# Attention with a gated feed-forward on one Trainium2 core: statistics turned at a unit's end and sent a unit sooner, row masks behind both kinds of scores

## The chip, the cores and the metric

The kernel runs on one core of a Trainium2 chip. A core has five engines with a queue each: TensorE (PE) multiplies matrices, VectorE (DVE) and ScalarE (ACT) work element by element and can read what PE wrote in PSUM, [...] and SyncE (SP) issues DMAs. [...] The metric is the time of one execution on the device, in microseconds (us); lower is better.

## What is computed

The reference, cut to what matters (16 sequences of 512 tokens, width 128, 16 heads with keys of 8 and values of 64 numbers, all fp32):

```python
xn = layernorm(x)
# attention
q = (xn @ Wq), k = (xn @ Wk), v = (xn @ Wv)          # split into 16 heads
scores = einsum('bhqd,bhkd->bhqk', q, k) / sqrt(8)
scores = where(causal, -inf, scores)                  # a query sees itself and earlier keys
attn = softmax(scores, axis=-1)
a = (attn @ v).reshape(B, T, 1024) @ Wo
# feed-forward
xr = mu_r * xn + (1 - mu_r) * shifted(xn)
xk = mu_k * xn + (1 - mu_k) * shifted(xn)
f = sigmoid(xr @ W_r.T) * (relu(xk @ W_k.T)**2 @ W_v.T)
out = x + a + f
```

## The kernel before

Every softmax is done with two kinds of scores. **Row scores** (tile `sm`, queries on the partitions) serve the statistics alone: DVE takes each row's negated maximum `negm`, ACT takes exp of the row with that maximum as bias and sums it into `z`, and takes the logarithm of the sums into `lz`. **Turned scores** (tile `sT`, keys on the partitions) serve the products with v: their matmul has 35 rows instead of 33, the two more being the statistics `negm - log z` of each query, split into a high and a low part (`mh`, `ml`) and written as two more rows of q. So `sT` comes out of PE already normalised, ACT takes its exp into `e`, POOL sets the diagonal blocks' masked half to zero, and PE multiplies with v (`weigh`, tile `av`), after which DVE copies the context out (`take_ctx`) and PE projects it (`project_out`, tile `po`).

The work is cut into units. A **group** is a batch's two pairs of heads and makes five units, t = 0 to 4, in which the blocks of 512 x 512 causal scores are dealt out [...] (`ROWS` L301 for the row scores, `KEYS` L309 for the turned ones, `WEIGHED` L317 for the products). A batch has four groups, so 20 units; 16 batches make 320. The function `unit_work(n)` (L531) issues one unit; it runs three groups' places at once. `now` is unit n, whose turned scores, exp and products are done. `stat_now` is unit n + 10 (`LEAD`), whose row sums ACT takes. `stat_next` is unit n + 11, whose row scores, masks and maxima are made.

Nothing but this order decides what runs when: `_InOrder` (L32) records each engine's instructions in program order, and each engine takes them one after another. In a unit the order is: send statistics (`put_stats` L409, four DMAs on POOL's queue that write `mh` and `ml` into q's rows), row scores (`rowscores` L328), their masks (`rowmask` L341, small bf16 matmuls that add -3e38 above the diagonal), turned scores (`scores` L424), the turn (`turn_stats` L398: PE transposes `lz` into `pm`, DVE makes `mh` and `ml`), a context copy, the maxima (`rowmax` L359), the row sums (`rowsum` L378) and, in a group's last statistics unit, the logarithm (`log_sums`), then exp and masks of `e` (`weights` L435), then side work and `weigh`. Side work comes from a table by unit number (`at` L492): the next batches' normalisation, projections of q, k and v, the feed-forward, the spreading of q and k over partitions by DMAs on SP's queue (`spread_qk` L232) and the output. Where t is 1, side work comes behind `weigh`, else ahead of it.

For a group whose row sums end in unit n (t = 4), the logarithm is taken in n, the subtraction `lz = negm - log z` (`sub_logs`, DVE) is the last piece of side work of n + 1, the turn is in n + 2 and the sending in n + 3. The turned scores that read the statistics begin in unit n + 6. With units of a batch numbered 0 to 19, the subtraction is in units 0, 5, 10 and 15, the turn in 1, 6, 11, 16, the sending in 2, 7, 12, 17.

Buffers that bind units to each other: `sm` has two PSUM buffers, so row scores wait for the row sums two units before; `sT` has one, so turned scores wait for the exp of the unit before; `av` has one, and the side products and `pm` share one tile `m`.

Side work that stands near the turns, in the middle of the run: unit 0 `ffn_r` (PE `pr`, DVE `e_sig`), unit 4 `y`, `deviation`, unit 5 a v projection, unit 9 the output `o` and `mix` (`xmix`), unit 10 the projection of q for the batch after next (DVE `qh`, `ql`), unit 14 a v projection and `mix`, unit 15 that of k (`kh`, `kl`). The last two batches have no batch after next and lack the q, k and normalisation pieces.

Of the kernel before, what the change touches and what calls it, by code (L numbers as in the profile page):

```python
# [47 lines left out]
def attn_ffn_kernel(  # L48
# [101 lines left out]
    def m_tile(name):  # L150
        n = lent[0] % 3 if lent else 0
        if lent:
            lent[0] += 1
        if n == 1:
            return ps_av.tile([P, T], FP, tag="av", name=name)
        if n == 2:
            return ps_st.tile([P, 2, 512], FP, tag="sT", name=name)[:, 0, :]
        return ps_m.tile([P, 512], FP, tag="m", name=name)
# [160 lines left out]
    def unit_of(n):  # L319

        n, t = divmod(n, UNITS)
        b, g = divmod(n, NPAIR // 2)
        return (b, g, t) if 0 <= b < B else None
# [4 lines left out]
    def rowscores(b, g, t):  # L328
        q, k = qs[b % 2], ks[b % 2]
        sm = sms[b, g, t] = ps_sm.tile([P, 2, 512], FP, tag="sm", name=f"sm_{b}_{g}_{t}")  # L330
        for w, i, to in ROWS[t]:
            n = (i + 1) * P
            for u in range(2):
                s = slice(64 * u, 64 * u + RS)

                pe.matmul(
                    sm[:, u, to : to + n], q[s, 2 * g + w, i * P : n], k[s, 2 * g + w, :n],
                    start=(to == 0), stop=False,
                )

    def rowmask(b, g, t):  # L341

        ends = [to + (i + 1) * P for _, i, to in ROWS[t]]
        step = ends[-1] - ends[0] or P
        for c in range(2):
            for u in range(2):
                s = slice(64 * u, 64 * u + 64)
                cols = sms[b, g, t][:, u, ends[0] - P :]
                if len(ends) > 1 and step > P:
                    cols = cols.rearrange("q (m k) -> q m k", k=P)[:, 0 :: step // P, 64 * c :]  # L350
                else:
                    cols = cols.rearrange("q (m k) -> q m k", k=P)[:, :, 64 * c :]
                pe.matmul(
                    cols, id64[s, c, :],
                    mask64[s, c : c + 1, 64 * c :].to_broadcast([64, len(ends), P - 64 * c]),
                    start=False, stop=(c == 1),
                )
# [20 lines left out]
    def rowsum(b, g, t):  # L378
        negm, z = stats[b, g]
        sm = sms.pop((b, g, t))  # L380
        for w, i, to in ROWS[t]:
            for u in range(2):
                cols = sm[:, u, to : to + (i + 1) * P]
                act.activation(
                    cols, cols, AF.Exp,
                    bias=negm[:, u, w, i : i + 1], accum_out=z[:, u, w, i : i + 1],
                )

    def log_sums(b, g):
        lz = stat.tile([P, 2, 2, NB], FP, tag="lz", name=f"lz_{b}_{g}")  # L390
        act.activation(lz, stats[b, g][1], AF.Ln)
        stats[b, g] += (lz,)
# [5 lines left out]
    def turn_stats(b, g):  # L398

        lz = stats.pop((b, g))[2]  # L400
        pm = m_tile(f"pm_{b}_{g}")[:, 0:P]
        pe.transpose(pm[0 : 4 * NB], lz.rearrange("q u p i -> q (u p i)"), ident)
        hi = stat.tile([4 * NB, P], FR, tag="mh", name=f"mh_{b}_{g}")
        lo = stat.tile([4 * NB, P], FR, tag="ml", name=f"ml_{b}_{g}")
        dve.tensor_copy(hi, pm[0 : 4 * NB])
        dve.tensor_tensor(lo, pm[0 : 4 * NB], hi.bitcast(FP), ALU.subtract)
        stats[b, g] = (hi, lo)

    def put_stats(b, g):  # L409

        for n, half in enumerate(stats.pop((b, g))):
            for u in range(2):
                r = 64 * u + RS + n
                pool.dma_start(
                    out=qs[b % 2].bitcast(FP)[r : r + 1, 2 * g : 2 * g + 2, :].rearrange(
                        "o p (i t) -> o (p i) t", t=P
                    ),
                    in_=half.bitcast(FP)[2 * NB * u : 2 * NB * u + 2 * NB],
                )
# [4 lines left out]
    def scores(b, g, t):  # L424
        q, k = qs[b % 2], ks[b % 2]
        st = sts[b, g, t] = ps_st.tile([P, 2, 512], FP, tag="sT", name=f"sT_{b}_{g}_{t}")
        for w, j, to in KEYS[t]:
            for u in range(2):
                s = slice(64 * u, 64 * u + RA)
                pe.matmul(  # L430
                    st[:, u, to : to + T - j * P], k[s, 2 * g + w, j * P : (j + 1) * P],
                    q[s, 2 * g + w, j * P : T], start=(to == 0), stop=(to + T - j * P == 512),
                )
# [28 lines left out]
    def take_ctx(b, p):  # L462
        c = ctxp.tile([P, T], FP, tag="ctx", name=f"ctx_{b}_{p}")
        dve.tensor_copy(c, avs.pop((b, p)))
        ctxs[b, p] = c
# [24 lines left out]
    todo, turns, puts = {}, {}, {}  # L490

    def at(n, f, *args):  # L492
        todo.setdefault(n, []).append((f, args))
# [4 lines left out]
    for b in range(B):  # L498
        n0 = b * per
        if b + 1 < B:  # L500
            r = 0 if b else 7
            at(n0 + r, ffn_r, b + 1)
            at(n0 + r + 1, ffn_exp, b + 1)
            for c, n in enumerate((3, 8, 13, 18) if b else (11, 13, 14, 18)):
                at(n0 + n, ffn_sig, b + 1, c)
            for m, n in enumerate((1 if b else 3, 5, 12, 13, 14, 16, 17, 18)):
                at(n0 + n, project_v, b + 1, m // 2, m % 2)
            at(n0 + 7, mix_prev, b + 1, 1)
            at(n0 + 9, mix, b + 1, 1)
            at(n0 + 11, ffn_k, b + 1)  # L510
            at(n0 + 19, ffn_out, b + 1)
            for m, n in enumerate((-3, -1, 0, 1, 4, 5, 5, 6) if b else (0, 0, 1, 1, 4, 5, 5, 6)):
                at(n0 + n, spread_qk, b + 1, *SPREAD[m], slice(0, NPAIR // 2))
            for m, n in enumerate((6, 9, 9, 10, 10, 11, 14, 14)):
                at(n0 + n, spread_qk, b + 1, *SPREAD[m], slice(NPAIR // 2, NPAIR))
        if b + 2 < B:
            at(n0 + 4, deviation, b + 2)
            for c in range(NB):
                at(n0 + (1, 1, 3, 3)[c], row_moments, b + 2, c)
                at(n0 + 4 + c // 2, normalise, b + 2, c)  # L520
            at(n0 + 6, transpose_xn, b + 2)
            at(n0 + 10, project_qk, b + 2, False)
            at(n0 + 15, project_qk, b + 2, True)
            at(n0 + 12, mix_prev, b + 2, 0)
            at(n0 + 14, mix, b + 2, 0)
        for p, n in enumerate((2, 3, 3, 4, 7, 8, 8, 9) if b < B - 1 else (-8, -7, -7, -6, -3, -2, 0, 3)):
            at(n0 + per + n, project_out, b, p)
        if b + 3 < B:
            at(n0 + 11, load_x, b + 3)

    def unit_work(n):  # L531
        now, stat_now, stat_next = (unit_of(n + m) for m in (0, LEAD, LEAD + 1))
        if n in puts:
            put_stats(*puts.pop(n))
        if stat_next:
            rowscores(*stat_next)
            rowmask(*stat_next)
        if now:
            scores(*now)
        if n in turns:  # L540
            turn_stats(*turns.pop(n))
        t = n % UNITS
        done = {0: (n - UNITS, 0), 2: (n - UNITS, 1)}.get(t)
        if done and unit_of(done[0]):
            b, g, _ = unit_of(done[0])
            take_ctx(b, 2 * g + done[1])
        if stat_next:
            rowmax(*stat_next)

        if stat_now:  # L550
            rowsum(*stat_now)
            b, g, kind = stat_now
            if kind == UNITS - 1:
                log_sums(b, g)
                at(n + 1, sub_logs, b, g)
                turns[n + 2] = puts[n + 3] = b, g
        if now:
            weights(*now)
        pieces = todo.pop(n, ())
        if t != 1:  # L560
            for f, args in pieces:
                f(*args)
        since, w, blocks = WEIGHED[t]
        if unit_of(n - since):
            b, g, _ = unit_of(n - since)
            for j in blocks:
                weigh(b, 2 * g + w, j, (t, j) in ((1, 3), (4, 3)))
        if t == 1:
            for f, args in pieces:
                f(*args)  # L570

    halves = {}

# [84 lines left out]
    for n in range(first - 1, B * per + 2):  # L658
        if n == -1:
            lent.clear()  # L660
        unit_work(n)
# [35 lines left out]
```

## Time and profile before

| | |
|---|---|
| median of 3 runs (lowest, highest) | 1035.7 us (1035.53, 1037.13) |
| the profiled execution | 1035.34 us, of it 1033.5 us span |
| TensorE clock granted | 0.976 |
| ACT: exp of `sT` into `e`, x320 | 324.5 us, 1014 ns each |
| ACT: exp of the rows, x1024, and reading out their sums | 513.4 us and 201.3 us |
| DVE: maxima, x448 | 397.2 us |
| PE: products with v, x2048 | 338.3 us (modelled ends) |
| PE: row masks, x1280 | 101.0 us (modelled ends, overlapping) |
| PE: `pm`, x64; DVE: `mh`, `ml`, x64 each | 17.8 us; 17.8 us, 17.8 us |
| POOL: sending `mh` and `ml`, x128 each | 70.7 us and 66.1 us, 4 KB each, 1.7 and 1.6 us to landing (median) |
| SP: spreads of q and k, x124 each | 128 KB each, 4.8 and 5.1 us to landing (median) |

The span runs from the first to the last instruction of the program; the profiled execution's own time is 1.84 us longer. All kernel code is recorded under line 42, the helper that opens the pools, so instructions are told apart by tile names: `sm<-k,q` are row scores, `sm<-mask,id` their masks, `sm<-sm,negm` the row sums, `e<-sT` the exp of turned scores. In a timeline a row gives start, duration, engine, operation, tiles and shapes, how many were merged, and in brackets how long the engine stood idle before it and what ended that.

### The profile page before, as it was taken

The numbers are of one execution on the slowest core, as the hardware profiler recorded it, in microseconds if no ns is written. First come the engines' busy times: TensorE is split into PE (matmuls) and PEld (weight loads), VectorE is DVE, ScalarE is ACT, GpSimd is POOL, SyncE is SP. The second block draws the span as 40 slices with busy tenths as digits, with TensorE's granted clock in tenths as the row PEclk, the third lists the DMA queues.
The fourth block names the chain that finished last, engine by engine and source line by source line (L and its number), as shares of the span: only waits on it lengthen the run. The fifth ranks groups of instructions, "written<-read, shape, count | busy, mean of one in ns | idle before, by whom it ended". The sixth has DMA issues, their size and how long they took to land.

```text
span 1033.5 us, 23971 instructions
## 1 busy us (share of the span) xinstructions
PE 976.3 (94%) x8771; PEld 527.6 (51%) x8771; DVE 793.9 (77%) x1316; ACT 923.9 (89%) x2449; POOL 514.1 (50%) x957
## 2 busy tenths in 40 slices
PE   3789999999999999999999999999999999999997
PEld 1344464555546455554645555464554646455454
DVE  4787879688887878787797877878787797877741
ACT  0788999899999999999899999999999999999982
POOL 4165454544646464463645545564464546444432
PEclk8778999999999999999999999999999999999999
DMA  7722515034250512525043252504324150432000
GB/s 193 136 28 49 99 34 112 15 73 84 59 98 19 114 29 73 85 59 98 3 108 50 58 100 50 97 14 107 50 58 90 34 102 4 110 37 48 3 12 11
DMA packets 59971, 67.17 MB, mean 65 GB/s; under 512 B 12928, under 2 KB 33024, under 8 KB 59856
## 3 DMA queue, kind: packets, MB, share of 16 engines
q1 hardware_dynamic: 48688, 61.89, 30.8%
q0 software_dynamic: 8640, 1.34, 1.1%
q10 hardware_dynamic: 2528, 2.43, 0.9%
q8 instruction: 70, 1.15, 0.5%
q14 instruction: 45, 0.37, 0.2%
HBM read 39.13 MB, written 25.17 MB: 62 GB/s over the span
## 4 chain that ended last, share of the span: by engine, by line
PE 49%; ACT 32%; DVE 11%; issue 4%; DMA 3%; POOL 1%; POOLq 0%; ACTq 0%
ACT sm L42 22%; PE av L42 14%; ACT e L42 10%; PE po L42 10%; PE sm L42 8%; PE sT L42 7%; DVE negm L42 6%; DMA q<-ml 3%; PE pv L42 3%; PE pq L42 2%; PE pk L42 2%; PE pr L42 1%; PE pm L42 1%; DVE mh L42 1%; DVE ml L42 1%
## 5 line engine op out<-in xcount | busy, mean ns | idle before, releaser
L42 ACT ACTIVATE sm<-sm,negm 128x384 f32<-128x384 f32 (+3 forms) x1024 | 513.4, 501 | 78.1 <-DVE negm L42 29.3
L42 DVE TENSOR_REDUCE negm<-sm 128x2 f32<-128x768 f32 (+3 forms) x448 | 397.2, 909 | 77.8 <-PE sm L42 77.8
L42 POOL TENSOR_SCALAR_AFFINE_SELECT e<-e 128x256 f32<-128x256 f32 x512 | 203.5, 416 | 457.1 <-ACT e L42 454.5
L42 ACT ACTIVATE e<-sT 128x1024 f32<-128x1024 f32 x320 | 324.5, 1014 | 18.5 <-PE sT L42 18.2
L42 PE MATMUL av<-e,v 128*64 128x512 f32 (+3 forms) x2048 | 338.3, 441 | 1.1 <-DVE ctx L42 0.5
L42 PEld LDWEIGHTS av<-e,v 128*64 128x64 f32 x2048 | 138.7, 138 | 166.5 <-issue 130.7
L42 ACT ACTIVATION_READ_ACCUMULATOR sm<-sm,negm 128x1 f32 x1024 | 201.3, 197 | 0.0
L42 PE MATMUL sT<-q,k 35*128 35x512 f32 (+3 forms) x1024 | 164.0, 366 | 23.5 <-ACT e L42 13.9
L42 PE MATMUL sm<-k,q 33*128 33x384 f32 (+3 forms) x1024 | 164.0, 378 | 8.3 <-ACT sm L42 8.3
L42 PEld LDWEIGHTS sm<-k,q 33*128 33x128 f32 x1024 | 83.1, 188 | 169.0 <-ACT sm L42 89.3
L42 PE MATMUL pv<-wv,xnT 128*64 128x512 f32 x512 | 139.0, 622 | 1.5 <-DVE ffn L42 0.9
L42 PE MATMUL po<-wo,ctx 128*64 128x128 f32 x2048 | 133.2, 277 | 1.6 <-DVE ctx L42 1.6
L42 PEld LDWEIGHTS po<-wo,ctx 128*64 128x64 f32 x2048 | 109.8, 137 | 18.6 <-issue 7.8
L42 PEld LDWEIGHTS sT<-q,k 35*128 35x128 f32 x1024 | 86.6, 189 | 49.0 <-ACT e L42 36.8
L42 PE MATMUL sm<-mask,id 64*128 64x128 bf16 (+2 forms) x1280 | 101.0, 236 | 0.0
L42 DVE COPY ctx<-av 128x512 f32<-128x512 f32 x128 | 87.3, 682 | 16.0 <-PE av L42 15.9
L42 DVE COPY v<-pv 128x512 f32<-128x512 f32 x128 | 86.0, 672 | 4.3 <-PE pv L42 0.6
L42 DVE CAST mh<-pm 16x128 fp32r<-16x128 f32 x64 | 17.8, 278 | 79.3 <-PE pm L42 79.3
L42 POOL DMA_DIRECT2D q<-mh x128 | 70.7, 555 | 12.9 <-DVE mh L42 7.6
L42 POOL DMA_DIRECT2D q<-ml x128 | 66.1, 521 | 0.0
L42 DVE RECIPROCAL sig<-e_sig 128x128 f32<-128x128 f32 x64 | 60.2, 941 | 0.0
L42 POOL TENSOR_SCALAR prev<-xnT,omm 128x512 f32<-128x512 f32 x32 | 50.2, 1567 | 14.0 <-DVE xmix L42 14.0
(65 smaller groups left out, 599.4 us busy)
## 6 DMA issues: line engine op xcount, KB each, us to landing
q<-q SPq DMA_DIRECT2D x124, 128.0 KB, 4.8
k<-k SPq DMA_DIRECT2D x124, 128.0 KB, 5.1
k<-kh SPq DMA_DIRECT2D x30, 256.0 KB, 2.6
x<-in_L_attn_x_dram SPq DMA_DIRECT2D x16, 256.0 KB, 2.9
q<-qh SPq DMA_DIRECT2D x16, 256.0 KB, 4.2
q<-ql SPq DMA_DIRECT2D x16, 256.0 KB, 4.3
out_dram<-o SPq DMA_DIRECT2D x16, 256.0 KB, 2.8
k<-kl SPq DMA_DIRECT2D x15, 256.0 KB, 2.0
```

What stands on the lines that cost most here:

```text
L42: return self._tc.keep_in_program_order(f(*args, **kwargs))
```

## The change

Three edits in `unit_work` and one in the side work's table. The row masks of unit n + 11 are issued behind the turned scores of unit n instead of ahead of them. The turn is issued at the very end of a unit, behind side work and products with v, and one unit sooner: in units 0, 5, 10 and 15 of a batch, the unit in which `sub_logs` stands. The sending comes one unit sooner too, at the start of units 1, 6, 11 and 16. And the spreads of q and k are given other units of the table.

```diff
-            for m, n in enumerate((-3, -1, 0, 1, 4, 5, 5, 6) if b else (0, 0, 1, 1, 4, 5, 5, 6)):
+            for m, n in enumerate((-1, -1, 0, 0, 4, 4, 5, 5) if b else (0, 0, 0, 0, 4, 4, 5, 5)):
                 at(n0 + n, spread_qk, b + 1, *SPREAD[m], slice(0, NPAIR // 2))
-            for m, n in enumerate((6, 9, 9, 10, 10, 11, 14, 14)):
+            for m, n in enumerate((8, 9, 9, 10, 10, 14, 14, 15)):
                 at(n0 + n, spread_qk, b + 1, *SPREAD[m], slice(NPAIR // 2, NPAIR))
...
         if n in puts:
             put_stats(*puts.pop(n))
+
         if stat_next:
             rowscores(*stat_next)
-            rowmask(*stat_next)
         if now:
             scores(*now)
-        if n in turns:
-            turn_stats(*turns.pop(n))
+        if stat_next:
+            rowmask(*stat_next)
...
                 log_sums(b, g)
                 at(n + 1, sub_logs, b, g)
-                turns[n + 2] = puts[n + 3] = b, g
+                turns[n + 1] = puts[n + 2] = b, g
...
         if t == 1:
             for f, args in pieces:
                 f(*args)
+        if n in turns:
+            turn_stats(*turns.pop(n))
```

## The prediction

> **What bounds the kernel now.** I read the page first, then the waits of the even stretch 100 to 990 us, then the timelines of ACT, DVE and PE around one turn of the statistics, and last the stretches of lost clock. A batch is 20 units and takes 60.2 us (unit 140's statistics-scores start at 484.21 us is disturbed, so I count from unit 160 at 547.81 to unit 180 at 607.99). I number units inside a batch 0 to 19; the turns before the change stand in units 1, 6, 11 and 16.
>
> The page gives the busy times:
> ```profile
> PE 976.3 (94%) x8771; PEld 527.6 (51%) x8771; DVE 793.9 (77%) x1316; ACT 923.9 (89%) x2449; POOL 514.1 (50%) x957
> ```
> PE looks like the bound, but its ends are modelled. The waits between engines (engine and tile that waited, what released it, us in total, times, longest) say more:
> ```profile
> DVE mh L42 <- PE pm L42: 68.8, 58, 3.2
> ...
> ACT sm L42 <- DVE negm L42: 20.8, 52, 0.9
> ...
> ACT e L42 <- PE sT L42: 5.1, 4, 2.3
> PE sT L42 <- DMA q<-ml: 4.5, 4, 2.0
> ```
> ACT waits in only two ways: 52 times for a row maximum, and a few times for scores whose statistics landed late. Between these it runs without a gap, so ACT sets the pace and PE waits about 0.5 us per group of five units, nearly all of it ahead of sT. ACT's timeline at unit 11 and 12 of batch 7 (start, us, then the idle time before in brackets):
> ```profile
> 523.34 1.01 ACT L42 ACTIVATE e<-sT 128x1024 f32<-128x1024 f32 x1
> 524.79 0.56 ACT L42 ACTIVATE sm<-sm,negm 128x384 f32<-128x384 f32 x1 [0.43 <-DVE negm L42]
> ```
> The missing maximum is that of unit 11. DVE's timeline shows why it is late:
> ```profile
> 516.53 1.29 DVE L42 TENSOR_REDUCE negm<-sm 128x2 f32<-128x768 f32 x2 [1.47 <-PE sm L42]
> 517.85 0.69 DVE L42 TENSOR_TENSOR o<-po,y 128x512 f32<-128x512 f32 x1
> 518.46 0.74 DVE L42 SCALAR_TENSOR_TENSOR xmix<-xnT,mus,prev 128x512 f32<-128x512 f32 x1
> 519.12 0.69 DVE L42 COPY ctx<-av 128x512 f32<-128x512 f32 x1
> 519.72 1.22 DVE L42 TENSOR_REDUCE negm<-sm 128x2 f32<-128x1024 f32 x1
> 520.85 0.68 DVE L42 CAST qh<-pq 128x512 fp32r<-128x512 f32 x1
> 521.56 0.69 DVE L42 TENSOR_TENSOR ql<-pq,qh 128x512 fp32r<-128x512 f32 x1
> 522.17 0.29 DVE L42 TENSOR_TENSOR lz<-negm,lz 128x16 f32<-128x16 f32 x1
> 522.97 0.28 DVE L42 CAST mh<-pm 16x128 fp32r<-16x128 f32 x1 [0.50 <-PE pm L42]
> 523.28 0.28 DVE L42 TENSOR_TENSOR ml<-pm,mh 16x128 fp32r<-16x128 f32 x1
> 523.49 1.27 DVE L42 TENSOR_REDUCE negm<-sm 128x2 f32<-128x768 f32 x2
> ```
> mh and ml stand ahead of the maximum and wait for pm. But lz, which pm turns, ends only at 522.47: from 516.53 to there DVE had no gap. And PE, on the same stretch:
> ```profile
> 521.74 0.50 PE L42 MATMUL sm<-k,q 33*128 33x384 f32 x4
> 522.09 0.34 PE L42 MATMUL sm<-mask,id 64*128 64x256 bf16 x4
> 522.24 0.48 PE L42 MATMUL sT<-q,k 35*128 35x256 f32 x4
> 522.65 0.28 PE L42 MATMUL pm<-ident,lz 128*16 128x128 f32 x1
> ```
> PE is through unit 10's products at 521.74, 0.73 us before lz is there. Today sm, masks and sT fill that time; the change puts pm exactly there. Last, unit 0 of batch 7, and the clock behind it (window; PE, PEld, DVE, ACT, POOL busy; clock; DMA share; GB/s):
> ```profile
> 486.76 0.96 PE L42 MATMUL sT<-q,k 35*128 35x512 f32 x2 [1.96 <-DMA q<-ml]
> ```
> ```profile
> 489.00:491.00 2.00, 2.00 (x10) 0.49 (x6) 0.57 (x2) 1.29 (x4) 0.33 (x1) 0.50 0.33 99
> ```
>
> [...] the maximum of unit 11 had its masks by 522.5 and still stood behind mh until 523.49. [...] here the 1.96 us stop was followed by a granted 0.50, while a stop of 1.27 us before the scores at 424.73 left it at 1.00. [...]
>
> **The change part by part.** Frame: the times of batch 7; ACT's free pace from one e's end to the next is 3.17, 2.39, 3.17, 2.40, 3.41 us for units 5k to 5k+4.
>
> 1. Row masks behind sT. The masks themselves cost PE 0.10 to 0.15 (516.15 to 516.30), unchanged in sum. But the maximum needs them: it starts 0.38 after the first mask (516.15, 516.53), and now sT (0.41: 516.30 to 516.71) stands between. So every maximum is possible 0.41 later than today, and where sT waits for the e before it (single sT buffer), the masks no longer fill that wait, which leaves PE 0.10 to 0.17 behind. Units whose maximum has slack of 0.7 us or more before ACT wants it hide this themselves; where DVE has no gap up to lz it passes on.
>
> 2. The turn (pm 0.21 of PE; mh and ml 0.60 of DVE) moves from the middle of unit 5k+1 to the end of unit 5k, behind the weigh. Same instructions. Gained: the maximum of 5k+1 no longer waits for a pm behind its own sT. Added: pm waits for lz of the same unit, and behind pm on PE stand the next unit's sm, sT and masks, that is ACT's next e and its next maximum. From pm's start to that maximum's start it is 0.21 + 0.35 (sm) + 0.41 + 0.38 = 1.35; mh and ml (pm + 0.31 + 0.60) hide in it.
>
>  Group at unit 10 (q of batch b+2 projected): unit 9's sm at 515.95 (0.15 behind), sT 516.30, masks 516.71, maximum 517.09 instead of 516.53. DVE is full, so lz ends at 522.47 + 0.56 = 523.03. pm 523.07, while PE is there at 521.89: 1.18 us stall. Maximum 524.42 to 525.69, row sums at 525.71 instead of 524.79: **+0.92**.
>  Group at unit 15 (k): today lz 537.05, PE free 536.72, maximum 538.47. sT waits for e; the masks behind it put unit 15's maximum at sT 533.92 + 0.79 = 534.71, so 535.92, kh and kl to 537.25, lz 537.43, pm 537.48 (stall about 0.65), maximum 538.83: **+0.37**.
>  Group at unit 0: lz 551.32, PE free 551.72. Unit 0's maximum at sT 548.90 + 0.79, ends 550.90, e_sig and lz to 551.7; no stall. pm 551.82, maximum 553.17 instead of 553.45; ACT's wait of 0.22 on average (3.3 us over 15 batches in unit 2) falls by **0.1**.
>  Group at unit 5: unit 4's maximum 501.46 becomes 501.87; y, mv, ve, ctx, maximum, v, lz have no gap, so lz 507.00, pm 507.05 against PE at 506.67; maximum 508.40 instead of 508.42: **0**.
>  Sum: +1.2 us per batch. Bounds: +0.6 if the maximum loses only sT's own 0.29 in the chain of waits and PE regains its 0.15; +1.6 if the unit 5 and unit 0 groups slip by 0.2 each too.
>  It holds for the 14 batches that project for b+2: +16.8. The last two have no q, k or xmix there and lose their ACT waits of about 0.23 four times: -1.
>
> 3. Sent a unit sooner. POOL's four DMAs (2.1 us) go ahead of the masking of unit 5k+1's e instead of 5k+2's; that e is first weighed two units later, so the place costs nothing (if not, up to 0.5 us a group). For the group read at unit 0 the sending comes about 1.8 us sooner (ml is ready only after pm at 537.5), and the lateness beyond the usual wait of 0.68 was at most 1.5. So ACT's waits for sT in units 0 and 1 (2.13, 2.33, 0.30, 0.14 us), half-clock stretches included, should go: -5. Bounds 0 and -5.4.
>
> 4. Spreads on SP: the same 16 of 128 KB per batch, regrouped; one q joins the three issued at unit 19 or 0. They are needed nine units after the first half and four after the second, 12 us or more against 5 us of landing: 0. [...] a spread in ml's way is inside the bounds of 3.
>
> Sum: +16.8 - 1 - 5 = +10.8 on the profiled execution's 1035.34 us (span 1033.5 and 1.84 around it) gives 1046.1; the median of the runs is 0.36 above it, so about 1047. Differences below 0.2% (2 us) can't be told from none here.
>
> **The rivals.**
> (a) Faster: the masks' delay is taken up. If PE stands early enough at units 4, 9 and 14 that the maximum still starts when today's does, lz stays where it is: unit 5's group gains its 0.43, unit 0's 0.22, unit 15's nothing, unit 10's still loses 0.36 (pm at 522.5). -0.3 x 14 - 1 - 5 = -10, 1026. For it: the DVE gaps of 0.81 and 1.47 us before these maxima. Against it: those gaps end exactly 0.38 after the mask, so PE decides them, and PE has no slack there. It decides from the point where unit 9's masks come within 0.1 us of today. At its best all of 20.8 + 5.1 us goes: 1010.
> (b) The new 1.2 us stop at unit 10 takes the clock down as the 1.96 us stop did; two such places cost ACT about 2 us each. 14 times gives 1075, half of them 1061. Against: 1.27 us did not do it.
> (c) The gains and losses meet: +0.4 per batch is +5.6 and meets the -6, so 1034 to 1038. For: step 2's lower bound of +0.6 is near.
> That the sending is not sooner at all, since lz holds it, would leave out the -5: 1052, inside the forecast's range.
>
> **How the numbers follow.** Forecast (1038 to 1058, at 1047) 0.56; (b) or longer stalls 0.11; (c) 0.07; (a) 0.26. Below 1020 I leave about 0.11 of (a), above 1061 about 0.08. Slower takes the forecast, (b) and a sliver of (c): 0.68; same 0.05; faster 0.27.
>
> **What would show it.** Right: PE idle before pm released by lz, near 1.2 us at unit 10 and 0.65 at unit 15; "ACT e waits for sT" growing from 5 us (unit 11); the wait of mh for pm falling to about 0.3 each; no PE wait for ml. Wrong: ACT's wait for negm falling below 10 us with no PE wait for lz, or a period below 60 us per batch.

## The result, and the profile after

The changed kernel takes 1032.49 us (median of 11 runs, 1031.75 to 1033.74) against 1037.13 us (11 runs, 1033.52 to 1038.42) for the one before: ratio 0.9961, 95% interval 0.9951 to 0.9971. It is faster by 0.4%, where 1.1% slower was forecast. Its profiled execution took 1032.25 us with a span of 1030.5, so 3.0 us of span are gone. ACT's work is the same:

```profile
PE 961.6 (93%) x8771; PEld 525.6 (51%) x8771; DVE 792.8 (77%) x1316; ACT 923.9 (90%) x2449; POOL 520.3 (50%) x957
```

The waits between engines in the same stretch as before, 100 to 990 us (total, times, longest):

```profile
DVE mh L42 <- PE pm L42: 29.3, 59, 0.7
...
PE pm L42 <- DVE lz L42: 20.0, 28, 1.0
...
ACT sm L42 <- DVE negm L42: 13.4, 27, 0.8
...
ACT e L42 <- PE sT L42: 7.1, 14, 0.7
```

mh's wait for pm fell from 68.8 to 29.3 us, PE's wait for lz is new, ACT waits less for maxima (20.8 to 16.1: the 13.4 shown and 2.7 in unit 7 that the view puts down to PE's xnTp; in batch 7 the maximum ended 0.1 us before ACT went on), and its wait for scores in unit 1 has become one in unit 11. The line for ml is gone. DVE's timeline around the same turn, units 9 to 11 of batch 7:

```profile
513.49 1.29 DVE L42 TENSOR_REDUCE negm<-sm 128x2 f32<-128x768 f32 x2 [1.14 <-PE sm L42]
...
516.55 1.22 DVE L42 TENSOR_REDUCE negm<-sm 128x2 f32<-128x1024 f32 x1
517.68 0.68 DVE L42 CAST qh<-pq 128x512 fp32r<-128x512 f32 x1
518.40 0.69 DVE L42 TENSOR_TENSOR ql<-pq,qh 128x512 fp32r<-128x512 f32 x1
519.00 0.17 DVE L42 TENSOR_TENSOR lz<-negm,lz 128x16 f32<-128x16 f32 x1
519.62 0.28 DVE L42 CAST mh<-pm 16x128 fp32r<-16x128 f32 x1 [0.45 <-PE pm L42]
519.94 0.28 DVE L42 TENSOR_TENSOR ml<-pm,mh 16x128 fp32r<-16x128 f32 x1
520.53 1.29 DVE L42 TENSOR_REDUCE negm<-sm 128x2 f32<-128x768 f32 x2 [0.31 <-PE sm L42]
```

and PE's:

```profile
512.48 0.50 PE L42 MATMUL sm<-k,q 33*128 33x384 f32 x4
512.82 0.45 PE L42 MATMUL sT<-q,k 35*128 35x384 f32 x4
513.11 0.34 PE L42 MATMUL sm<-mask,id 64*128 64x256 bf16 x4
513.38 1.09 PE L42 MATMUL po<-wo,ctx 128*64 128x128 f32 x16
...
516.94 1.46 PE L42 MATMUL av<-e,v 128*64 128x512 f32 x8
519.32 0.27 PE L42 MATMUL pm<-ident,lz 128*16 128x128 f32 x1 [0.92 <-DVE lz L42]
```

The reader is to see two things. PE stands idle for 0.92 us ahead of pm at unit 10's end, where 1.18 was forecast, and the next maximum comes after it. But the masks start only 0.29 us after sT (512.82 to 513.11), not 0.41, so unit 9's maximum starts 1.01 us after its row scores (512.48 to 513.49) where it was 0.73 before (515.80 to 516.53).

Where the 3 us went is best seen from the times between the last exp of one batch and of the next, read from the two traces (the lead-in is what runs before batch 0's own units):

| us | before | after | difference |
|---|---|---|---|
| lead-in and batch 0 | 119.78 | 121.05 | +1.3 |
| batches 1 to 13 | 792.48 | 790.16 | -2.3 |
| of these, the shortest | 60.16 | 60.70 | +0.5 |
| of these, the longest | 63.60 | 61.36 | -2.2 |
| batch 14 | 60.29 | 58.88 | -1.4 |
| batch 15 and end | 60.94 | 60.46 | -0.5 |

An undisturbed batch, one whose statistics landed in time, became slower, 60.17 to 60.73. Before, batches 2 and 7 took 63.24 and 63.60 us and several others 60.4 to 61.2; after, batches 1 to 12 lie between 60.70 and 60.76 and only batch 13 takes 61.36. Against 13 times 60.17 the kernel before lost 10.3 us to such batches. From 489 to 491 us, where the kernel before was granted a clock of 0.50, the changed one was granted 1.00 (the clock is the third number from the end, then come DMA share and GB/s):

```profile
489.00:491.00 2.00, 2.00 (x24) 1.05 (x20) 1.61 (x4) 1.97 (x6) 1.78 (x5) 1.00 0.41 121
```

### The profile page after: what moved, and what is told of

It reads as the page before. It is cut to its first block, busy times and chain, and to the rows that moved or that the text cites. A ratio compares the mean times of both kernels' runs of the same rounds, so it can differ in the third digit from the quotient of the medians.

```text
span 1030.5 us, 24120 instructions
## 1 busy us (share of the span) xinstructions
PE 961.6 (93%) x8771; PEld 525.6 (51%) x8771; DVE 792.8 (77%) x1316; ACT 923.9 (90%) x2449; POOL 520.3 (50%) x957
## 4 chain that ended last, share of the span: by engine, by line
PE 57%; ACT 19%; DVE 17%; issue 6%; POOL 1%; DMA 0%; ACTq 0%; DVEq 0%; POOLq 0%
PE av L42 16%; ACT sm L42 13%; PE sm L42 12%; PE po L42 10%; DVE negm L42 7%; PE sT L42 7%; ACT e L42 6%; PE pv L42 6%; DVE sig L42 2%; PE pr L42 1%; DVE v L42 1%; PE pm L42 1%; PE pkv L42 1%; DVE xmix L42 1%; PE xnTp L42 1%
## 5 line engine op out<-in xcount | busy, mean ns | idle before, releaser
L42 POOL TENSOR_SCALAR_AFFINE_SELECT e<-e 128x256 f32<-128x256 f32 x512 | 208.2, 426 | 418.2 <-ACT e L42 416.0
L42 PE MATMUL sT<-q,k 35*128 35x512 f32 (+3 forms) x1024 | 146.5, 338 | 4.5 <-ACT e L42 4.3
L42 PE MATMUL pv<-wv,xnT 128*64 128x512 f32 x512 | 141.5, 632 | 6.9 <-DVE v L42 5.3
L42 PEld LDWEIGHTS po<-wo,ctx 128*64 128x64 f32 x2048 | 109.8, 137 | 17.1 <-issue 9.7
L42 PEld LDWEIGHTS sT<-q,k 35*128 35x128 f32 x1024 | 90.2, 187 | 28.6 <-ACT e L42 22.6
L42 PEld LDWEIGHTS <-id 64*128 64x128 bf16 x1280 | 40.1, 97 | 29.6 <-issue 15.7
```

The costliest lines, as they stand in the source:

```text
L42: return self._tc.keep_in_program_order(f(*args, **kwargs))
```

## The experiments

Each row is one kernel with its ratio to the kernel before on the same chip; "batch" is the time of an undisturbed batch, "idle" what ACT stood still in the profiled execution per batch (mean of batches 1 to 13) in gaps over 0.06 us, by the unit of the batch in which it ends; units 0 to 3, where late statistics show, are left out.

| kernel | median us | ratio, 95% interval | batch | ACT idle in units |
|---|---|---|---|---|
| before | | 1 | 60.17 | 7: 0.46, 12: 0.43, 17: 0.33 |
| changed | 1032.5 | 0.9961 (0.9951 to 0.9971) | 60.73 | 7: 0.21, 11: 0.49, 12: 0.51, 17: 0.48 |
| 1 masks ahead | 1022.1 | 0.9843 (0.9816 to 0.9870) | 59.88 | 11: 0.59 |
| 2 masks behind alone | 1043.3 | 1.0049 (1.0027 to 1.0070) | 60.78 | 7: 0.59, 12: 0.69, 17: 0.49 |
| 3 sent as before | 1041.7 | 1.0040 (1.0019 to 1.0061) | 60.77 | 7: 0.37, 11: 0.48, 12: 0.51, 17: 0.48 |
| 4 spreads as before | 1032.3 | 0.9949 (0.9931 to 0.9967) | 60.81 | 7: 0.16, 11: 0.47, 12: 0.51, 17: 0.48 |
| 5 lz first | 1027.0 | 0.9888 (0.9863 to 0.9912) | 60.61 | 7: 0.09, 11: 0.47, 12: 0.51, 17: 0.48 |
| 6 lz first, masks ahead | 1016.0 | 0.9780 (0.9755 to 0.9805) | 59.90 | 11: 0.57, 16: 0.10 |
| 7 spreads alone | 1037.8 | 1.0000 (0.9978 to 1.0023) | 60.16 | 7: 0.46, 12: 0.44, 17: 0.33 |
| 8 as 6, q and k off the turn | 1000.1 | 0.9645 (0.9614 to 0.9677) | 58.83 | none |
| 9 as 1, q and k off the turn | 1004.6 | 0.9687 (0.9652 to 0.9722) | 58.77 | none |
| 10 changed, q and k off the turn | 1014.3 | 0.9783 (0.9752 to 0.9815) | 59.42 | 7: 0.18, 12: 0.38 |

**1. The masks ahead again** in the changed kernel.

```diff
-        if now:
-            scores(*now)
         if stat_next:
             rowmask(*stat_next)
+        if now:
+            scores(*now)
```

> The changed kernel with the row masks ahead of the turned scores again (turn, sending and spreads stay changed). Theory A (what costs in the undisturbed batches is that the maxima start 0.28 us later, which DVE passes on to lz without a gap, and that pm at a unit's end waits for lz): lz comes 0.28 us sooner in units 0, 5, 10, 15, PE's wait for lz falls from about 0.9 to 0.6 us at unit 10, an undisturbed batch takes about 60.2 us instead of 60.73, the whole 1024 to 1028 us. Theory B (the order of masks and turned scores is neutral, only pm's wait costs): 1031 to 1034 us, batch 60.7. Theory C (the masks behind are what lets e start in time with the turn at the end): slower, 1035 us or more.

Measured 1022.1 us and 59.88 us a batch, better than any theory said. ACT's waits for maxima in units 7, 12 and 17 are all gone; what is left is the wait for scores in unit 11, behind pm. Theories B and C fall: the order of masks and turned scores costs the changed kernel 0.85 us a batch. The waits of experiment 1 in the 130 to 890 us stretch:

```profile
PE pm L42 <- DVE lz L42: 15.2, 26, 0.7
...
ACT e L42 <- PE sT L42: 7.7, 13, 0.6
```

**2. The masks behind alone** in the kernel before (the same two calls moved, nothing else).

> The kernel before with only the row masks moved behind the turned scores. Theory A: the turn's maximum is held by pm anyway and pm stands where it stood, so only the groups in which lz has no reserve (unit 10) lose, 0.1 to 0.3 us per batch, and the late statistics stay: 1037 to 1042 us. Theory B (neutral): 1035 to 1038. Theory C (it gains by itself): under 1034.

1043.3 us, slower by 0.3 to 0.7%. The batch goes from 60.17 to 60.78, twice what theory A said: I had counted only on unit 10's lz, but ACT waits longer in all three groups. With experiment 1 the four corners are measured: the masks behind cost 0.61 us a batch with the old turn and 0.85 with the new; the new turn gains 0.29 with masks ahead and 0.05 with masks behind.

**3. Sent as before**: the changed kernel with the sending (DMAs issued on GpSimd, POOL) one unit later again, the turn where the change put it.

```diff
-                turns[n + 1] = puts[n + 2] = b, g
+                turns[n + 1] = puts[n + 3] = b, g
```

> The changed kernel with the sending put back to three units behind the row sums (two after the turn), the turn itself staying at the unit's end. Theory A (the gain over the kernel before is that statistics sent a unit sooner no longer land late in unit 0): the irregular batches come back, with PE waiting for ml in unit 0; undisturbed batches stay near 60.7 us, the whole 1037 to 1044 us. Rival D (the spreads' new units made the landing punctual): stays 1031 to 1034, all batches 60.7.

1041.7 us with batches from 60.76 to 62.25 us: the irregular batches are back, and so is PE's wait (same stretch):

```profile
PE sT L42 <- DMA q<-ml: 3.5, 5, 0.9
```

In the trace 6.7 us lie between the end of ml's last issue and the first turned scores of unit 0 that read it, 6.6 in the least of the kernel before, 8.7 in the changed one. SP's spreads of the next batch are issued in that time. Of the irregular batches none has half clock here, and the longest is 62.25 us.

**4. Spreads as before** in the changed kernel, and **7. spreads alone** in the kernel before: the two lines of the side work's table exchanged.

> The changed kernel with the spreads in the units of the kernel before. Theory A: no difference, 1031 to 1034 us, every undisturbed batch 60.7. Rival D: the irregular batches of the kernel before come back, 1036 to 1044 us, with PE waiting for ml in unit 0.

> The kernel before with only the spreads in their new units. Theory A (spreads' units play no part): 1035 to 1042 us, undisturbed batches 60.2, and batches of 61 to 63.6 us with statistics landing late remain. Rival D (the spreads' units make them punctual): no irregular batch, 1026 to 1031 us.

1032.3 us with every batch of 1 to 12 at 60.8; and 1037.8 us, ratio 1.0000, with batches of up to 64.97 us and 8.4 us of waits for ml from 130 to 890 us (3.6 in the kernel before). The spreads' new units do nothing by themselves, and rival D falls. What makes the statistics punctual in the changed kernel is that they are sent a unit sooner.

Experiment 7 also shows what the clock adds. In its batch 7 PE stood for ml longer than in any batch of the kernel before, and the clock stayed at 1.00 (the stop, then the stretch behind it):

```profile
488.92 1.00 PE L42 MATMUL sT<-q,k 35*128 35x512 f32 x2 [2.08 <-DMA q<-ml]
```

```profile
489.00:491.00 2.00, 1.94 (x20) 1.32 (x22) 0.02 (x1) 1.47 (x5) 0.32 (x1) 1.00 0.22 48
```

That batch took 62.17 us, where batch 7 of the kernel before, with a stop of 1.96 us and 3.41 us at half clock, took 63.60. Batch 2 of experiment 7, with 2.10 and 6.83 us, took 64.97. An estimate from these three: 3.41 us at half clock lengthen a batch by some 1.4 us.

**5 and 6. lz first**: the subtraction ahead of the unit's maximum, in the changed kernel and in experiment 1's.

```diff
-                at(n + 1, sub_logs, b, g)
+                subs[n + 1] = b, g
...
+        if n in subs:
+            sub_logs(*subs.pop(n))
         if stat_next:
             rowmax(*stat_next)
```

> The changed kernel with the subtraction that makes lz issued on DVE ahead of the unit's maximum and side work instead of behind them; masks stay behind. Theory A (pm waits for lz because lz stands behind the maximum and the projections' copies): PE's wait for lz (some 22 us over the run) goes, ACT's wait for scores in unit 11 (0.48 us a batch) and for the maxima in units 12 and 17 go or shrink below 0.2; a batch takes 59.0 to 59.9 us, the whole 1010 to 1022 us. Theory B (pm at a unit's end costs through its place on PE and its tile, not through lz): PE's wait stays, batch 60.5 or more, 1030 or more.

> As the last, and the row masks ahead of the turned scores again. Theory A: the only wait that the masks-ahead version still had (ACT's for scores in unit 11, 0.59 us a batch) goes, ACT runs without a gap, a batch takes its own 58.7 to 59.3 us, the whole 1004 to 1014 us, faster than every kernel so far. Theory B: no better than masks ahead alone, 1020 to 1024 us, batch 59.9.

Both missed: the batch is 60.61 and 59.90, as without the edit. DVE and PE of experiment 5 at unit 10 show why:

```profile
572.93 0.16 DVE L42 TENSOR_TENSOR lz<-negm,lz 128x16 f32<-128x16 f32 x1
573.01 1.22 DVE L42 TENSOR_REDUCE negm<-sm 128x2 f32<-128x1024 f32 x1
574.15 0.68 DVE L42 CAST qh<-pq 128x512 fp32r<-128x512 f32 x1
574.86 0.69 DVE L42 TENSOR_TENSOR ql<-pq,qh 128x512 fp32r<-128x512 f32 x1
576.00 0.28 DVE L42 CAST mh<-pm 16x128 fp32r<-16x128 f32 x1 [0.45 <-PE pm L42]
```

```profile
573.33 1.46 PE L42 MATMUL av<-e,v 128*64 128x512 f32 x8
575.70 0.27 PE L42 MATMUL pm<-ident,lz 128*16 128x128 f32 x1 [0.91 <-DVE ql L42]
```

lz is there at 573.1, and pm still starts at 575.70, now released by ql. pm and the projection pq lie in the same PSUM tile `m`, which has one buffer, so pm may not be written until ql has read pq. In the changed kernel lz (to 519.17) had only been the last of two conditions, 0.1 us behind the other (ql, to 519.09). Theory A is mended (A2): what stands between PE and pm is the copies out of the side product before it. The totals did fall (1027.0 and 1016.0), but in the profiled executions the lead-in and batch 0 make most of that: 117.6 us in experiment 5 against 121.05 in the changed kernel, 116.1 in 6 against 117.8 in 1. There the theory holds: the changed kernel's PE stood 2.02 us ahead of the pm at 76.59, released by lz, experiments 1 and 9 have the same stop at 74.20 and 75.79, and experiments 5, 6 and 8, with lz first, have none there. (Experiment 1's trace is of the fastest of its six runs, 1017.0 us, so it can't show all of the 6 us between the medians of 1 and 6.)

**8, 9 and 10. q and k off the turn**: the projection of q changes places with a v projection of unit 12, that of k with one of unit 17, so that one copy instead of two reads `m` before pm; in experiment 6's kernel, in 1's and in the changed one.

```diff
-            for m, n in enumerate((1 if b else 3, 5, 12, 13, 14, 16, 17, 18)):
+            for m, n in enumerate((1 if b else 3, 5, 10, 13, 14, 15, 16, 18) if b + 2 < B else (1 if b else 3, 5, 12, 13, 14, 16, 17, 18)):
...
-            at(n0 + 10, project_qk, b + 2, False)
-            at(n0 + 15, project_qk, b + 2, True)
+            at(n0 + 12, project_qk, b + 2, False)
+            at(n0 + 17, project_qk, b + 2, True)
```

> The version with lz first and masks ahead, and the projections of q and k swapped with v projections so that they stand in units 12 and 17 and v in 10 and 15. Theory A2 (pm at the unit's end waits for the tile m that it shares with the projection before it: ql read it last in unit 10, kl in unit 15; lz was the last to come only by the order on DVE): one copy of 0.6 us reads m instead of two of 1.3, PE's wait before pm and ACT's 0.57 us in unit 11 go, a batch takes 59.0 to 59.4 us instead of 59.9, the whole 1005 to 1011 us. Rival (pm is held by something that goes with the unit, not with q's copies): batch stays 59.9, 1014 to 1018 us.

> The same swap in the masks-ahead version, with lz behind the side work as in the changed kernel. Theory A2: the copy of v and then lz are done by the time that PE reaches pm, 0.7 us sooner than ql was; batch 59.0 to 59.5, the whole 1006 to 1017 us: lz first adds nothing. Rival: 59.9 and 1017 to 1024.

> The same swap in the changed kernel itself, masks behind. Theory A2: the stalls of units 10 and 15 shrink, ACT's 0.48 us in unit 11 goes, but the maxima stay 0.28 us later and units 12 and 17 may keep a part of their 0.49: batch 59.5 to 60.2, the whole 1014 to 1026 us. Rival: 60.7 and 1031 to 1034.

A2 holds in all three; the batch is shorter than was expected in each. PE in experiment 8, at unit 10:

```profile
558.00 1.08 PE L42 MATMUL pv<-wv,xnT 128*64 128x512 f32 x4
558.91 1.46 PE L42 MATMUL av<-e,v 128*64 128x512 f32 x8
560.30 0.28 PE L42 MATMUL pm<-ident,lz 128*16 128x128 f32 x1
560.51 0.51 PE L42 MATMUL sm<-k,q 33*128 33x384 f32 x4
```

pm follows the products without a gap. In batches 1 to 13 ACT has no gap left above 0.06 us, with lz first or not: 58.83 and 58.77 us a batch, near the 58.67 that ACT's free paces of the prediction sum to (four times 14.54, and 0.51 for the sigmoid's exp). With masks behind, 59.42 and waits for maxima remain: without the stall the masks still cost 0.65 us a batch. The swap takes DVE's second copy out of the turn's unit as well as the second reader of `m`. That the tile and not DVE's load held pm rests on experiment 5, where DVE had lz ready and pm waited for ql; a pm with a tile of its own was not tried. Experiment 8, at 1000.1 us, beats both kernels of the case; between it and 9 the batches are equal, and their profiled executions differ by 5.9 us in lead-in and batch 0 (115.8 and 121.7).

The swap also changed the landing of ml, which no expectation had named. With k's projection in unit 17 instead of 15, SP issues the copies and spreads of k behind the sending. In the kernel before, batch 7, ml's issue ended at 478.72 behind SP's spreads, and it landed 8.4 us later; in experiment 8 it ended at 460.13, SP's queue started on k at 463.27, and ml landed 1.1 us later. The DMA engines' share in the two stretches (last but one number), first the kernel before, then experiment 8:

```profile
479.00:482.00 3.00, 3.00 (x28) 1.45 (x29) 2.68 (x4) 2.97 (x7) 0.86 (x3) 1.00 1.12 131
```

```profile
459.00:461.00 2.00, 2.00 (x22) 0.89 (x18) 1.12 (x4) 1.97 (x5) 1.91 (x5) 1.00 0.06 8
```

In batches 1 to 14 of experiments 8, 9 and 10 this group's ml lands 1.0 to 2.0 us after its issue. So the sooner sending is one cure for the late statistics, and keeping the spreads off it looks like another; the old sending with k's projection moved was not tried.

## Why the prediction was wrong, point by point

- **The bound** was right: ACT's free pace, broken once per group by a maximum. Experiments 8 and 9 reach that pace.
- **Step 1, masks behind sT**: the mechanism was right, its size was not. The term "sT (0.41: 516.30 to 516.71) stands between" was mis-sized. 0.41 is the distance from sT to the 64-column products that followed it. From sT to masks it is 0.29 at unit 9 and 0.23 to 0.35 over the changed kernel's trace; the rest came behind the masks instead (513.11 to 513.38 is 0.27 where it was 0.15). So maxima moved by 0.28 us, not 0.41 to 0.56. The chain of waits had shown sT with 0.29, which the text kept as a lower bound and did not take. The supposed regular 0.15 us of PE behind was not there either, as sT now seldom waits for e (4.3 us in the whole run; 13.9 before). Experiment 1 weighs the term alone: rival (a), with the masks' delay at nothing, was computed at -0.3 us a batch, and the changed kernel with the masks ahead measured 59.88 against 60.17, -0.29. The forecast of +1.2 had thus priced the masks' delay at 1.5 us a batch, and it cost 0.85. (The close agreement at -0.3 is of the sums and in part luck: rival (a) counted a gain of 0.22 at unit 0, where undisturbed batches had no wait to lose.)
- **Step 2, the turn**: by group, in undisturbed batches, ACT's wait changed by +0.54 at unit 10 (forecast +0.92), +0.15 at unit 15 (+0.37), -0.26 at unit 5 (0); unit 0's group had no wait to lose (forecast -0.1). Sum +0.4 against +1.2, and +0.56 by the length of the batch. The rest is that a batch now has four such waits instead of three, and a unit with one is longer by 0.11 us more than the gap (unit 17 before: 0.33 of gap, 0.44 longer), since ACT's instructions otherwise overlap by about that much (an exp that ends at 424.09 before the change has the next row sum starting at 423.99). It is the first term's error carried through: each lz came 0.28 late instead of 0.4 to 0.56. The sign in the undisturbed batches was right, and PE's stall was 0.92 at unit 10 and 0.52 at unit 15 where 1.18 and 0.65 were forecast. The signs that the prediction named for its mechanism appeared: PE idle ahead of pm, ACT's wait for scores in unit 11 (7.1 us in all), no wait for ml.
- **The reason given for the stall** was half of it. "pm waits for lz of the same unit" is what the profile names, but experiment 5 shows that ql's reading of tile m held pm just as long. The prediction itself named the shared tile nowhere, though the section on the kernel has it.
- **Step 3, sent a unit sooner**: the direction was right, "-5" was mis-sized. It counted ACT's waits for scores in units 0 and 1. Against a regular batch the irregular ones had lost 10.3 us: a late landing also makes the maxima of unit 2 late (2.8 us of ACT's waits in batches 1 to 13, which the prediction had put under the turn), and twice the clock was halved for 3.4 us. After the change batches 1 to 13 exceed 13 times 60.73 by 0.7 us. Experiments 3, 4 and 7 show that the sooner sending did it.
- **Step 4, the spreads**: right, 0.
- **The last two batches**: -1.9 us measured, -1 forecast.
- **Rival (b)**, the clock: the changed kernel keeps 1.00 from 93.2 to 1028.4 us, through all its stops at units 10 and 15. The reason given against it was weak. The stop before 424.73 reads 1.08 us in the timeline, not 1.27, and in experiment 7 stops of 2.10 and 2.08 us were followed by 0.50 and by 1.00.
- **The sum** so turned over: +16.8 became +7.3 (13 times 0.56), -5 became -9.6, -1 became -1.9, and the lead-in with batch 0 added 1.3: -2.9, against -3.0 of span. Rival (a), whose point was that unit 9's masks come within 0.1 us of before, did not happen; it was near (c), "the gains and losses meet", and then the sending carried it over.

What stays open: what sets ml's landing in unit 0's group of the kernel before, which took 5.4 to 8.4 us after the issue in batches 1 to 14, now within the 6.6 us there were and now not; and what sets the length of the lead-in, which differs from kernel to kernel by several microseconds and does not follow its half-clock stretches (experiment 9: 17.1 us of them, 121.7 us in all; experiment 8: 27.3 and 115.8).

## What to carry to other kernels

A wait for two conditions hides the second one: before moving an instruction to a place, list everything that it needs there, the buffer that it writes included, because the profile names only the last to come (here lz, to 519.17, and not ql, to 519.09). Here the distance from one matmul to the next differed by the pair (from sT 0.41 us to a 64-column product, 0.29 to the masks), so in an order written by hand a delay is better priced by the smallest distance seen than by the one that stood beside it. And price an irregularity by comparing whole periods with an undisturbed one, not by the waits that carry its name.

## What the runs showed of the hardware that was not expected

- From the first matmul of sT (35 rows, fp32) to the next instruction's start it was mostly 0.41 to 0.43 us in the kernel before, where a product with 64-column weights followed (0.50 before pk and pr), and 0.23 to 0.35 in the changed one, where the bf16 masks followed. At unit 9 the sum over sT and masks stayed 0.56.
- Stops of PE of nearly one length were followed by different granted clocks. In the kernel before, 1.80 us (before 181.30) and 1.96 us (before 486.76) were followed by 3.41 us at 0.50; in experiment 7, 2.10 us (before 180.95) were followed by 6.83 us at 0.50 and 2.08 us (before 488.92) by none. What decides between the two was not shown.
- 4 KB transfers with a median of 1.6 us to landing took 5.4 to 8.4 us after their issue in unit 0's group of the kernel before, beside SP's 128 KB spreads (DMA engines' share 1.12 from 479 to 482 us). Sent sooner, with 8.7 us to spare, they took 3.8 to 5.5 in batches 1 to 14 and PE did not wait; with the spreads issued behind them (experiments 8 to 10) they took 1.0 to 2.0.
